# State-space mixer: front and output of a batch in pieces, one to a state; an own PSUM bank for rows of B; exponentials kept in du

## The chip, the cores and the metric

The kernel runs on one core of a Trainium2 chip. The metric is the device time of one execution in microseconds (us). The kernel is a chain of eight layers; the change lies in the seventh, a state-space mixer (`l3_attn`), and in the first step of the eighth.

## The reference

Input is x of shape 8 x 512 x 256 (batch, time, width), float32. Each layer computes `x = x + layernorm(f(layernorm(x)))`. For the seventh layer f is a selective state-space mixer with 512 channels and 16 states:

```
xr = x @ W_in.T                      # 256 -> 2 x 512
u, res = xr[..., :512], xr[..., 512:]
u = silu(causal_conv4(u) + b_conv)   # per channel
dt, B, C = split(u @ W_xproj.T, 16, 16, 16)
delta = softplus(dt @ W_dt.T + b_dt)
A = -exp(A_log)
for t:                               # per channel d and state n
    h = exp(delta*A) * h + delta*B*u
    y[d] = sum_n h[d, n] * C[n]
y = (y + u*D) * silu(res)
f = y @ W_out.T
```

The eighth layer is a mixture of experts whose routing starts with the layernorm of every batch of x.

## The kernel before

All activations lie with 128 partitions. In the mixer channels are on partitions in four chunks c, and the 512 times of a batch lie along the free axis. The loop runs over `order`, the pairs (batch b, state n), 8 x 16. For each pair:

- ACT writes `dA = exp(delta*A)` for each chunk into one of two PSUM banks (`pA`, L1727),
- DVE scans over time, `h = dA*h + dB` (L1730), into one of six buffers of two chunks,
- POOL multiplies h by the row of C, in place, two chunks at a time (L1733),
- PE adds h into the four banks `py` with an identity matrix (`summed`, L1701); this is issued one state late.

`dB = du*B`, where du = delta*u, is made two states ahead by `inputs`. For even states PE spreads the row of B over the partitions with a matmul into PSUM (`pb`, L1673) and DVE multiplies (L1676). For odd states a DMA on SP's queue brings the row from DRAM (L1680) and POOL multiplies (L1681). The row of C always comes by DMA (L1670).

`front(b)` makes what a batch needs. Its steps are the norm (`norm_act`, ACT writes xn, L160; PE transposes it, L146), four times a projection (`project_in`, `pi`, L1609), copy to `xc` (L1620), convolution by matmuls with diagonal matrices (`pc`, L1623) and bias (L1626), then Silu of u (L1628), the projection to dt, B and C (L1633), softplus in four chunks (ACT L1651 to L1655, DVE L1657 to L1659), and du on POOL (L1662). It is a generator: one step is issued behind each state of the batch before, and the rest ahead of state 14.

The boundary between batches is in state 0 of the next one. There stand the gate of the batch that has ended (`gate`, DVE, L1691), the first term of y (L1739), the output projection and the residual (`out`: `project_out`, L193, and `add_norm`), and the projections and Silu of the next `sr = silu(res)` (L1745, L1746). In `add_norm` DVE takes statistics (L105, L107, L113 to L115, L170), ACT normalizes (L177) and POOL adds to X (L182).

Two PSUM banks (`pmm`) serve the norm's transposes, projections, convolutions, softplus, rows of B and the output projection; two hold dA and four y. The instructions of an engine run in their order. That order is set by a scheduler, which takes the program's order as priority but moves work forward when by its own estimate it is ready. So work of the next layer can stand inside the mixer: the statistics of routing do (`norm` with L105, L118, L90 to L96).

Of the kernel before, what the change touches and what calls it, by code (L numbers as in the profile page):

```python
# [45 lines left out]
class Kern:  # L46


    def __init__(self, ctx, tc, i):
        self.ctx, self.tc, self.nc, self.i = ctx, tc, tc.nc, i  # L50
        nc = self.nc
        self.const = ctx.enter_context(tc.tile_pool(name="const", bufs=1))
        self.xpool = ctx.enter_context(tc.tile_pool(name="xres", bufs=1))
        self.wpool = ctx.enter_context(tc.tile_pool(name="wts", bufs=1))
        self.small = ctx.enter_context(tc.tile_pool(name="small", bufs=3))
        self.dram = ctx.enter_context(tc.tile_pool(name="dram", bufs=1, space=DRAM))
        self.C = self.const.tile([P, 384], F32, name="C")
        nc.sync.dma_start(out=self.C, in_=i["consts"][:, 0:384])
        self.ident = self.C[:, C_ID:C_ID + 128]
        self.caus = self.C[:, C_CAUS:C_CAUS + 128]  # L60
        self.up = self.C[:, C_UP:C_UP + 128]
        self.ones = self.const.tile([1, 128], F32, name="ones")
        nc.vector.memset(self.ones, 1.0)
        self.XA = self.xpool.tile([P, NB, NT, D], F32, name="X")
        self.X = [self.XA[:, b] for b in range(NB)]
        self.W = {}

        self.log_exp = False
        self.eps = self.const.tile([P, 1], F32, name="eps")
        nc.vector.memset(self.eps, LN_EPS)  # L70
# [55 lines left out]
    def norm(self, b, pool):  # L126

        nc = self.nc
        x = self.X[b]
        mv, r = self.stats([x[:, n, :] for n in range(NT)], "ln")  # L130
        xn = pool.tile([P, NT, D], F32, tag="xn", name=f"xn{b}")
        for n in range(NT):
            nc.vector.tensor_scalar(
                xn[:, n, :], x[:, n, :], mv[:, n, 0:1], r[:, n:n + 1], ALU.subtract, ALU.mult)
        return xn
# [15 lines left out]
    def norm_act(self, b, pool):  # L151

        nc = self.nc
        x = self.X[b]
        mv, r = self.stats([x[:, n, :] for n in range(NT)], "ln")
        nb = self.small.tile([P, NT], F32, tag="lnb", name="lnb")
        nc.vector.scalar_tensor_tensor(nb, mv[:, :, 0], -1.0, r, ALU.mult, ALU.mult)
        xn = pool.tile([P, NT, D], F32, tag="xn", name=f"xn{b}")
        for n in range(NT):
            nc.scalar.activation(  # L160
                xn[:, n, :], x[:, n, :], AF.Identity, bias=nb[:, n:n + 1], scale=r[:, n:n + 1])
        return xn

    def add_norm(self, b, ys, pool, tag="yn", halves=(), parts=1):
# [6 lines left out]
        t = pool.tile([P, NT, D], F32, tag=tag, name=f"yn{b}")  # L171
# [1397 lines left out]
def l3_attn(K):  # L1569

    nc, tc = K.nc, K.tc
# [5 lines left out]
    with ExitStack() as es:  # L1579
# [4 lines left out]
        pmm = pool("pm", 2, space=PSUM)  # L1584
# [21 lines left out]
        def project_in(b, c, xT):  # L1606
            ps = pmm.tile([P, L], F32, tag="mm", name=f"pi{b}_{c}")
# [6 lines left out]
        def front(b, res):  # L1614
            xT = K.norm_T(
                b, s1, pmm, "mm", xn=K.norm_act(b, s1), dst=s1.tile([P, 2, L], F32, tag="xT", name=f"xT{b}"))
            yield
            u = s1.tile([P, 4, L], F32, tag="u", name=f"u{b}")
            for c in range(4):
                nc.scalar.copy(xc[:, 3:], project_in(b, c, xT))  # L1620
# [5 lines left out]
                nc.scalar.activation(u[:, c, :], pc, AF.Identity, bias=W[:, c, M_BC:M_BC + 1])  # L1626
                yield
            nc.scalar.activation(flat(u), flat(u), AF.Silu)  # L1628
            K.log_exp_tables()
            yield  # L1630
# [12 lines left out]
            dl = s2.tile([P, 4, L], F32, tag="dl", name=f"dl{b}")  # L1643
            for c in range(4):
                ps = pmm.tile([P, L], F32, tag="mm", name=f"pd{b}_{c}")
# [3 lines left out]
                e = s2.tile([P, L], F32, tag="e", name=f"e{b}_{c}")  # L1649
                lg = s2.tile([P, L], F32, tag="lg", name=f"lg{b}_{c}")  # L1650
                nc.scalar.activation(e, ps, AF.Abs, bias=bd)  # L1651
                nc.scalar.activation(dl[:, c, :], ps, AF.Relu, bias=bd)
                nc.scalar.activation(e, e, AF.Exp, scale=-1.0)
                nc.scalar.activation(ps, e, AF.Identity, bias=1.0)
                nc.scalar.activation(lg, ps, AF.Ln)  # L1655

                nc.vector.scalar_tensor_tensor(ps, ps, -1.0, e, ALU.add, ALU.subtract)  # L1657
                nc.vector.tensor_tensor(ps, lg, ps, ALU.subtract)
                nc.vector.tensor_tensor(dl[:, c, :], ps, dl[:, c, :], ALU.add)  # L1659
                yield  # L1660
            du = s2.tile([P, 4, L], F32, tag="du", name=f"du{b}")
            nc.gpsimd.tensor_tensor(flat(du), flat(dl), flat(u), ALU.mult)  # L1662
            res.update(xT=xT, u=u, dl=dl, du=du, xd=xd,
                       rows=xd_d.rearrange("(j n) t -> n j t", j=2))

        def inputs(b, n):
            du, xd, rows = res[b]["du"], res[b]["xd"], res[b]["rows"]
            dB = s3.tile([P, 4, L], F32, tag="dB", name=f"dB{b}_{n}")
            C = s4.tile([P, L], F32, tag="C", name=f"C{b}_{n}")
            nc.sync.dma_start(out=C, in_=rows[n, 1].partition_broadcast(P))  # L1670
            if n % 2 == 0:
                pb = pmm.tile([P, L], F32, tag="mm", name=f"pb{b}_{n}")
                nc.tensor.matmul(  # L1673
                    pb, lhsT=K.ident[0:48, 16 + n:17 + n].to_broadcast([48, P]), rhs=xd,
                    start=True, stop=True)
                nc.vector.tensor_tensor(  # L1676
                    dB, du, pb[:, None, :].to_broadcast([P, 4, L]), ALU.mult)
            else:
                B = s2.tile([P, L], F32, tag="B", name=f"B{b}_{n}")
                nc.sync.dma_start(out=B, in_=rows[n, 0].partition_broadcast(P))  # L1680
                nc.gpsimd.tensor_tensor(  # L1681
                    dB, du, B[:, None, :].to_broadcast([P, 4, L]), ALU.mult)
            return dB, C

        def out(b, yT):
            K.project_out(
                b, [(yT[:, c, :], W[:, c, M_OUT:M_OUT + D]) for c in range(4)], pmm, "mm", s1, tag="xn")
# [16 lines left out]


# [5 lines left out]
        ready = {k: inputs(*k) for k in order[:2]}  # L1711
        py = sr = last = None
        nxt = iter(())
        for k, (b, n) in enumerate(order):
            if n == 0:
                nxt = front(b + 1, res[b + 1]) if b + 1 < NB else iter(())
                dl, u = res[b]["dl"], res[b]["u"]
            if n == NS - 2:
                for _ in nxt:
                    pass  # L1720
            dB, C = ready.pop((b, n))
            if k + 2 < len(order):
                ready[order[k + 2]] = inputs(*order[k + 2])
            hs = []
            for c in range(4):
                dA = pA.tile([P, L], F32, tag="dA", name=f"dA{b}_{n}_{c}")
                nc.scalar.activation(dA, dl[:, c, :], AF.Exp, scale=A[:, c, n:n + 1])  # L1727
                if c % 2 == 0:
                    hs.append(s6.tile([P, 2, L], F32, tag="h", name=f"h{b}_{n}_{c}"))
                nc.vector.tensor_tensor_scan(  # L1730
                    hs[-1][:, c % 2, :], dA, dB[:, c, :], 0.0, ALU.mult, ALU.add)
            for h in hs:
                nc.gpsimd.tensor_tensor(h, h, C[:, None, :].to_broadcast([P, 2, L]), ALU.mult)  # L1733
            summed(last)
            if n == 0:
                yT = gate(b - 1, py, sr) if b else None
# [4 lines left out]
                if b:  # L1741
                    out(b - 1, yT)
                sr = s1.tile([P, 4, L], F32, tag="sr", name=f"sr{b}")
                for c in range(4):
                    nc.scalar.copy(sr[:, c, :], project_in(b, 4 + c, res[b]["xT"]))  # L1745
                nc.scalar.activation(flat(sr), flat(sr), AF.Silu)  # L1746
                K.log_exp_tables()
            last = (py, hs, n)
            next(nxt, None)
        summed(last)  # L1750
        out(NB - 1, gate(NB - 1, py, sr))
# [4 lines left out]
def l3_ffn(K):  # L1756
# [18 lines left out]
    with ExitStack() as es:  # L1775
# [60 lines left out]
        def route(b, sb):  # L1836

            xn = K.norm(b, sb)
# [343 lines left out]
```

## Time and profile before

| what | value |
|---|---|
| median of 3 runs (lowest, highest) | 5109.19 us (5106.86, 5115.65) |
| profiled execution, its time | 5105.01 us |
| its span | 5103.3 us |
| granted TensorE clock, mean | 0.933 |
| mixer, from the first scan to the last matmul of y | 3346.9 to 4447.1 us |
| POOL, DVE, PE busy between 3343 and 4437 us | 918, 838, 932 us of 1094 |

A line of the groups has line, engine, operation, result and operands, count, then busy time and mean ns of one, and the idle time just ahead of it with what ended that. A line of a timeline has start, length, engine, line, operation, count, and in brackets the idle time ahead of it with its releaser. A line of waits has who waited for whom, the sum in us, how many times, and the longest.

### The profile page before, as it was taken

The numbers are of one execution on the slowest core, as the hardware profiler recorded it, in microseconds if no ns is written. First come the engines' busy times: TensorE is split into PE (matmuls) and PEld (weight loads), VectorE is DVE, ScalarE is ACT, GpSimd is POOL, SyncE is SP. The second block draws the span as 40 slices with busy tenths as digits, with TensorE's granted clock in tenths as the row PEclk, the third lists the DMA queues.
The fourth block names the chain that finished last, engine by engine and source line by source line (L and its number), as shares of the span: only waits on it lengthen the run. The fifth ranks groups of instructions, "written<-read, shape, count | busy, mean of one in ns | idle before, by whom it ended". The sixth has DMA issues, their size and how long they took to land.

```text
span 5103.3 us, 56570 instructions
## 1 busy us (share of the span) xinstructions
PE 4394.7 (86%) x18804; PEld 2694.8 (53%) x18804; DVE 3045.6 (60%) x8229; ACT 1958.5 (38%) x3835; POOL 1854.5 (36%) x1209
## 2 busy tenths in 40 slices
PE   8745788999895698899999999888888888799998
PEld 3334675555553697455555555433333333368884
DVE  6999746465778212666666543277777787751115
ACT  5411333434333233444444434365455555421112
POOL 0001212444433343211111110078778888803321
PEclk9877898999998899899999999999999999999999
DMA  4287421000001696000000000011111111126763
GB/s 114 79 198 177 130 64 56 5 5 9 5 14 40 171 249 173 5 5 5 5 5 5 1 21 1 1 54 45 42 44 44 50 46 42 56 71 226 235 206 103
DMA packets 401528, 357.89 MB, mean 70 GB/s; under 512 B 209394, under 2 KB 334020, under 8 KB 400676
## 3 DMA queue, kind: packets, MB, share of 16 engines
q1 hardware_dynamic: 373236, 305.83, 21.6%
q0 software_dynamic: 16320, 31.65, 2.2%
q10 hardware_dynamic: 11680, 16.80, 1.0%
q8 instruction: 149, 2.44, 0.2%
q14 instruction: 143, 1.17, 0.1%
HBM read 287.87 MB, written 66.09 MB: 69 GB/s over the span
## 4 chain that ended last, share of the span: by engine, by line
PE 37%; DVE 18%; issue 4%; POOL 4%; ACT 3%; DMA 1%; DVEq 0%; POOLq 0%; ACTq 0%; SPq 0%
DVE h L1730 7%; PE T L1432 5%; PE gb L1809 4%; DVE junk L1402 3%; PE h L1243 3%; PE g L1558 3%; PE y L1701 3%; PE yb L1823 2%; PE py L193 2%; DVE dB L1676 2%; PE pc L1623 2%; PE y L1254 2%; POOL h L1733 2%; PE o L1422 2%; PE pi L1609 1%
## 5 line engine op out<-in xcount | busy, mean ns | idle before, releaser
L1733 POOL TENSOR_TENSOR h<-h,C 128x1024 f32<-128x1024 f32 x256 | 595.8, 2354 | 175.6 <-DVE h L1730 141.9
L1701 PE MATMUL y<-h,C 128*128 128x512 f32 x1024 | 531.4, 660 | 107.1 <-POOL h L1733 107.1
L1730 DVE TENSOR_TENSOR_SCAN h<-dA,dB 128x512 f32<-128x512 f32 x512 | 589.0, 1203 | 29.4 <-ACT dA L1727 11.7
L1727 ACT ACTIVATE dA<-dl,A 128x512 f32<-128x512 f32 x512 | 352.5, 691 | 410.8 <-DVE h L1730 404.7
L1701 PEld LDWEIGHTS y<-h,C 128*128 128x128 f32 x1024 | 201.2, 208 | 414.5 <-issue 222.3
L938 POOL TENSOR_SCALAR p<-p,rs 128x128 f32<-128x128 f32 (+3 forms) x256 | 276.0, 1087 | 385.5 <-DVE rs L937 225.9
L1435 ACT ACTIVATE PT<-T 128x256 f32<-128x256 f32 (+3 forms) x512 | 212.1, 438 | 416.1 <-PE T L1432 396.0
L182 POOL TENSOR_TENSOR X<-X,yn 128x1024 f32<-128x1024 f32 (+1 forms) x80 | 154.1, 1932 | 590.3 <-ACT yn L177 529.3
L1397 PE MATMUL S<-KT,qz 128*128 128x512 f32 (+3 forms) x1024 | 326.0, 455 | 38.4 <-ACT qz L1385 16.9
L1432 PE MATMUL T<-qz,KT 128*128 128x512 f32 (+3 forms) x1024 | 318.1, 447 | 6.3 <-DVE mx L1402 4.2
L1437 POOL TENSOR_SCALAR_AFFINE_SELECT PT<-PT 128x512 f32<-128x512 f32 x128 | 81.8, 640 | 604.2 <-ACT PT L1435 599.8
L1681 POOL TENSOR_TENSOR dB<-du,B 128x2048 f32<-128x2048 f32 x64 | 289.6, 4525 | 0.1
L1402 DVE CUSTOM_DVE_ANT_0 junk<-S,mask 128x256 f32<-128x256 f32 (+3 forms) x512 | 249.8, 488 | 46.7 <-PE S L1397 2.6
L1397 PEld LDWEIGHTS S<-KT,qz 128*128 128x128 f32 x1024 | 178.5, 191 | 158.8 <-DVE mx L1402 36.7
L1809 PE MATMUL gb<-xbT,w_b 128*128 128x256 f32 (+1 forms) x1472 | 255.3, 332 | 1.0 <-ACT ts L2013 0.6
L1676 DVE TENSOR_TENSOR dB<-du,pb 128x2048 f32<-128x2048 f32 x64 | 145.4, 2273 | 167.2 <-PE pb L1673 117.5
L1815 DVE TENSOR_TENSOR hTb<-sb,gb 128x512 f32<-128x512 f32 x71 | 48.8, 687 | 325.4 <-PE gb L1809 325.4
L1809 PEld LDWEIGHTS gb<-xbT,w_b 128*128 128x128 f32 x1472 | 230.2, 191 | 23.1 <-ACT ts L2013 0.8
L1432 PEld LDWEIGHTS T<-qz,KT 128*128 128x128 f32 x1024 | 168.2, 191 | 121.5 <-issue 70.4
L936 ACT ACTIVATE p<-p,nm 128x128 f32<-128x128 f32 (+3 forms) x256 | 143.8, 563 | 198.5 <-DVE nm L932 193.3
L1248 ACT ACTIVATE hT<-h,w_l_ffn 128x128 f32<-128x128 f32 x384 | 109.8, 368 | 220.4 <-PE h L1243 220.4
L1243 PE MATMUL h<-xgT,w 128*128 128x128 f32 x1536 | 185.0, 279 | 0.0
(505 smaller groups left out, 9125.8 us busy)
## 6 DMA issues: line engine op xcount, KB each, us to landing
w_b<-l3f_w SPq DMA_DIRECT2D x138, 512.0 KB
w<-l1f_w SPq DMA_DIRECT2D x48, 1024.0 KB
C<-xdd SPq DMA_DIRECT2D x128, 256.0 KB
B<-xdd SPq DMA_DIRECT2D x64, 256.0 KB
w<-l1f_w SPq DMA_DIRECT2D x48, 256.0 KB
toep<-l0fd SPq DMA_DIRECT2D x32, 320.0 KB
X<-x SPq DMA_DIRECT2D x16, 512.0 KB
toep<-l0fd SPq DMA_DIRECT2D x32, 256.0 KB
```

The costliest lines, as they stand in the source:

```text
L938: nc.gpsimd.tensor_scalar(p[:, 0:n], p[:, 0:n], rs, None, ALU.mult)
L1243: nc.tensor.matmul(ph[:, j, :], lhsT=w1[:, s, c, m * P:(m + 1) * P], rhs=xgT[:, c, :], start=(c == 0), stop=(c == 1))
L1397: nc.tensor.matmul(ps[:, 0:n], lhsT=QZ[:, j, qt * P:n], rhs=KT[:, g, 0:n], start=True, stop=True)
L1402: nc.vector.tensor_tensor_reduce(out=junk[:, 0:n], in0=tiles[j][:, 0:n], in1=mask[:, L - n:L], scale=1.0, scalar=-3.0e38, op0=ALU.add, op1 ...
L1432: nc.tensor.matmul(ps[:, 0:n], lhsT=KT[:, g, kt * P:(kt + 1) * P], rhs=QZ[:, j, kt * P:L], start=True, stop=True)
L1676: nc.vector.tensor_tensor(dB, du, pb[:, None, :].to_broadcast([P, 4, L]), ALU.mult)
L1681: nc.gpsimd.tensor_tensor(dB, du, B[:, None, :].to_broadcast([P, 4, L]), ALU.mult)
L1701: nc.tensor.matmul(py[2 * j + c], lhsT=K.ident, rhs=h[:, c, :], start=False, stop=(n == NS - 1))
L1727: nc.scalar.activation(dA, dl[:, c, :], AF.Exp, scale=A[:, c, n:n + 1])
L1730: nc.vector.tensor_tensor_scan(hs[-1][:, c % 2, :], dA, dB[:, c, :], 0.0, ALU.mult, ALU.add)
L1733: nc.gpsimd.tensor_tensor(h, h, C[:, None, :].to_broadcast([P, 2, L]), ALU.mult)
L1809: nc.tensor.matmul(ps[:, q, :], lhsT=ww[:, k, (c + q) * P:(c + q + 1) * P], rhs=xT[:, k, :], start=(k == 0), stop=(k == 1))
```

## The change

Front and output of a batch are cut into 15 pieces, and one is issued in each of the states 1 to 15, between the second and the third scan (`among`). Pieces 1 to 5 are the norm, projections and convolutions; 6 is both Silu and the projection to dt, B and C; 7 to 12 softplus and du; 13 and 15 the projections for `sr`. The output of the batch before goes into pieces 7, 9 and 10. In state 0 only the gate and the first term of y are left.

`pmm` has one bank; the other becomes `pB`, for rows of B, half of the softplus projections, the `sr` projections and the halves of the output. Rows are asked for three states ahead (`rows_of`), and the products are made two ahead (`product`). The exponentials of softplus are kept in the place of du, so Abs and Exp of all chunks come ahead of the logarithms, and du is then written over them in four parts. xn lies in half of u. `sr` has two buffers, and its Silu is taken together with that of the next u. In the last batch the pieces take the statistics of routing for batches 0 to 6, each held on DVE behind a `fence`, and `norm` in the eighth layer uses them.

```diff
+    def fence(self):
+        t = self.small.tile([P, 1], F32, tag="fence", name="fence")
+        return self.tc.keep_in_program_order(self.nc.vector.memset(t, 0.0)).ins
-    def norm(self, b, pool):
+    def norm(self, b, pool, known=None):
-        mv, r = self.stats([x[:, n, :] for n in range(NT)], "ln")
+        mv, r = known or self.stats([x[:, n, :] for n in range(NT)], "ln")
...
-        pmm = pool("pm", 2, space=PSUM)
+        pmm = pool("pm", 1, space=PSUM)
+        pB = pool("pb", 1, space=PSUM)
...
-        def front(b, res):
+        def front(b, res, sr=None):
+            u = s1.tile([P, 4, L], F32, tag="u", name=f"u{b}")
+            xn = K.norm_act(b, s1, u[:, 2:4, :].rearrange("p c t -> p (c t)").rearrange(
+                "p (n d) -> p n d", n=NT))
             xT = K.norm_T(
+                b, s1, pmm, "mm", xn=xn, dst=s1.tile([P, 2, L], F32, tag="xT", name=f"xT{b}"))
+            nc.scalar.copy(xc[:, 3:], project_in(b, 0, xT))
             yield
             for c in range(4):
-                nc.scalar.copy(xc[:, 3:], project_in(b, c, xT))
                 pc = pmm.tile([P, L], F32, tag="mm", name=f"pc{b}_{c}")
...
+                if c < 3:
+                    nc.scalar.copy(xc[:, 3:], project_in(b, c + 1, xT))
                 yield
-            nc.scalar.activation(flat(u), flat(u), AF.Silu)
+            for t in (sr, u):
+                if t is not None:
+                    nc.scalar.activation(flat(t), flat(t), AF.Silu)
             K.log_exp_tables()
-            yield
...
             for c in range(4):
-                ps = pmm.tile([P, L], F32, tag="mm", name=f"pd{b}_{c}")
+                pl, tag = (pmm, "mm") if c < 2 else (pB, "pb")
+                ps = pl.tile([P, L], F32, tag=tag, name=f"pd{b}_{c}")
...
-                nc.scalar.activation(e, ps, AF.Abs, bias=bd)
+                nc.scalar.activation(du[:, c, :], ps, AF.Abs, bias=bd)
                 nc.scalar.activation(dl[:, c, :], ps, AF.Relu, bias=bd)
-                nc.scalar.activation(e, e, AF.Exp, scale=-1.0)
-                nc.scalar.activation(ps, e, AF.Identity, bias=1.0)
+                if c % 2:
+                    e = flat(du[:, c - 1:c + 1, :])
+                    nc.scalar.activation(e, e, AF.Exp, scale=-1.0)
+                if c == 1:
+                    yield
+            for c in range(4):
+                ps = pmm.tile([P, L], F32, tag="mm", name=f"pl{b}_{c}")
+                lg = s1.tile([P, L], F32, tag="e", name=f"lg{b}_{c}")
+                nc.scalar.activation(ps, du[:, c, :], AF.Identity, bias=1.0)
                 nc.scalar.activation(lg, ps, AF.Ln)
+                yield
-                nc.vector.scalar_tensor_tensor(ps, ps, -1.0, e, ALU.add, ALU.subtract)
+                nc.vector.scalar_tensor_tensor(ps, ps, -1.0, du[:, c, :], ALU.add, ALU.subtract)
                 nc.vector.tensor_tensor(ps, lg, ps, ALU.subtract)
                 nc.vector.tensor_tensor(dl[:, c, :], ps, dl[:, c, :], ALU.add)
-                yield
-            nc.gpsimd.tensor_tensor(flat(du), flat(dl), flat(u), ALU.mult)
+                nc.gpsimd.tensor_tensor(du[:, c, :], dl[:, c, :], u[:, c, :], ALU.mult)
+            for c in range(4):
+                if c % 2 == 0:
+                    yield
+                    if c:
+                        yield
+                nc.scalar.copy(res["sr"][:, c, :], project_in(b, 4 + c, xT, pB, "pb"))
...
+        def product(b, n, B):
+            dB = s3.tile([P, 4, L], F32, tag="dB", name=f"dB{b}_{n}")
+            m = 4 if n else 1
+            for c in range(0, 4, m):
+                (nc.gpsimd if n % 2 else nc.vector).tensor_tensor(
+                    dB[:, c:c + m, :], res[b]["du"][:, c:c + m, :],
+                    B[:, None, :].to_broadcast([P, m, L]), ALU.mult)
+            return dB
...
         def out(b, yT):
-            K.project_out(
-                b, [(yT[:, c, :], W[:, c, M_OUT:M_OUT + D]) for c in range(4)], pmm, "mm", s1, tag="xn")
+            t = s1.tile([P, NT, D], F32, tag="xn", name=f"yn{b}")
+            for half in range(2):
+                ps = pB.tile([P, 2, D], F32, tag="pb", name=f"po{b}_{half}")
...
+                nc.scalar.copy(t[:, 2 * half:2 * half + 2, :], ps)
+                yield
+            K.add_norm(b, [t[:, n, :] for n in range(NT)], s1, t=t)
...
+        def among(b, yT):
+            sr = res[b]["sr"]
+            behind = out(b - 1, yT) if b else iter(())
+            if b + 1 < NB:
+                for n, _ in enumerate(front(b + 1, res[b + 1], sr), 1):
+                    if n in (7, 9, 10):
+                        next(behind, None)
+                    yield
+            else:
+                for _ in behind:
+                    yield
+                nc.scalar.activation(flat(sr), flat(sr), AF.Silu)
+                K.log_exp_tables()
+                for d in range(NB - 1):
+                    yield
...
+                    with tc.issue_after(K.fence()):
+                        m, t = K.stats([K.X[d][:, n, :] for n in range(NT)], "ln")
+                        nc.vector.tensor_copy(mv, m)
+                        nc.vector.tensor_copy(r, t)
...
         for k, (b, n) in enumerate(order):
-            if n == NS - 2:
-                for _ in nxt:
-                    pass
-            if k + 2 < len(order):
-                ready[order[k + 2]] = inputs(*order[k + 2])
             for c in range(4):
...
+                if n and c == 1:
+                    next(nxt, None)
+                    if n == NS - 1:
+                        for _ in nxt:
+                            pass
+            if k + 2 < len(order):
+                ahead = order[k + 2]
+                dBs[ahead] = product(*ahead, rows[ahead][0])
+            if k + 3 < len(order):
+                rows[order[k + 3]] = rows_of(*order[k + 3])
...
             if n == 0:
...
-                if b:
-                    out(b - 1, yT)
-                sr = s1.tile([P, 4, L], F32, tag="sr", name=f"sr{b}")
-                for c in range(4):
-                    nc.scalar.copy(sr[:, c, :], project_in(b, 4 + c, res[b]["xT"]))
-                nc.scalar.activation(flat(sr), flat(sr), AF.Silu)
-                K.log_exp_tables()
+                nxt = among(b, yT)
```

## The prediction

> **What bounds the kernel now.** I read the page first (groups, idle times), then the waits inside the mixer (3343 to 4437 us), then the timelines of POOL and DVE over one boundary between two batches. Only the state-space mixer and the first microseconds after it are touched; the rest of the span is taken over unchanged.
>
> The groups (busy, mean ns | idle before, releaser):
>
> ```profile
> L1733 POOL TENSOR_TENSOR h<-h,C 128x1024 f32<-128x1024 f32 x256 | 595.8, 2354 | 175.6 <-DVE h L1730 141.9
> L1730 DVE TENSOR_TENSOR_SCAN h<-dA,dB 128x512 f32<-128x512 f32 x512 | 589.0, 1203 | 29.4 <-ACT dA L1727 11.7
> L1681 POOL TENSOR_TENSOR dB<-du,B 128x2048 f32<-128x2048 f32 x64 | 289.6, 4525 | 0.1
> ```
>
> POOL's work for one batch is 595.8/8 + 289.6/8 + 4.5 (du) + 2.35 (adding to X) = 117.5 us. DVE's: 64 scans at a pitch of 1.13 are 72, eight products at 2.2 are 18, softplus 8, gate 2.5, statistics with their waits about 5: 105. PE's, at full clock: 232 matmuls of 512 columns at 0.43, 32 of 256 at 0.215: 107. A batch takes, from one first gate to the next (DVE timeline):
>
> ```profile
> 3471.65 0.69 DVE L1691 TENSOR_TENSOR sr<-y,sr 128x512 f32<-128x512 f32 x1 [1.60 <-PE y L1701]
> ...
> 3615.53 0.69 DVE L1691 TENSOR_TENSOR sr<-y,sr 128x512 f32<-128x512 f32 x1 [1.59 <-PE y L1701]
> ```
>
> 143.9 us; over the six periods up to the gate at 4331.94 it is 143.4. So POOL is the nearest bound and idles 26 us a batch. Where, its timeline says:
>
> ```profile
> 3624.72 9.28 POOL L1733 TENSOR_TENSOR h<-h,C 128x1024 f32<-128x1024 f32 x4
> 3636.77 4.65 POOL L1733 TENSOR_TENSOR h<-h,C 128x1024 f32<-128x1024 f32 x2 [2.77 <-DVE onb L170]
> 3641.37 2.36 POOL L182 TENSOR_TENSOR X<-X,yn 128x1024 f32<-128x1024 f32 x1
> 3643.68 4.54 POOL L1681 TENSOR_TENSOR dB<-du,B 128x2048 f32<-128x2048 f32 x1
> 3666.36 9.28 POOL L1733 TENSOR_TENSOR h<-h,C 128x1024 f32<-128x1024 f32 x4 [18.14 <-DVE h L1730]
> ```
>
> 18.1 of the 26.4 us are one hole just behind the boundary, in which POOL waits for a scan. DVE over the same stretch:
>
> ```profile
> 3643.76 1.41 DVE L105 BATCH_NORM_STATS2 lnst<-X 128x6 f32<-128x256 f32 x4 [4.92 <-POOL X L182]
> 3646.84 1.39 DVE L115 SCALAR_TENSOR_TENSOR lnw<-lnh,lny 128x4 f32<-128x4 f32 x1 [1.66 <-ACT xn L160]
> ...
> 3661.46 2.29 DVE L1676 TENSOR_TENSOR dB<-du,pb 128x2048 f32<-128x2048 f32 x1 [12.01 <-PE pb L1673]
> 3663.79 9.02 DVE L1730 TENSOR_TENSOR_SCAN h<-dA,dB 128x512 f32<-128x512 f32 x8
> ```
>
> DVE waits 4.92 us for X (statistics that belong to the next layer's routing, pulled forward by the scheduler), 1.66 for xn, and 12.01 for the row of B, whose matmul stands on PE behind projections, transposes and the first convolution, all sharing two PSUM banks. The waits of the mixer in total:
>
> ```profile
> POOL h L1733 <- DVE h L1730: 141.9, 28, 18.2
> ...
> DVE dB L1676 <- PE pb L1673: 117.5, 17, 16.3
> ...
> DVE dB L1676 <- POOL du L1662: 49.7, 8, 6.4
> DVE lnst L105 <- POOL X L182: 29.5, 6, 4.9
> ```
>
> **The change, part by part.** (1) Rows of B get the bank pB and are asked for three states ahead, not two. This takes away most of the 12.0 us and the later waits for pb (3.9 us at 3676). A two-pass pb matmul costs 0.86 us as before. (2) Projections, convolutions, softplus and output projection become pieces 1 to 15, one behind the second scan of each state. Instruction counts on PE stay; ACT gains two copies of the output halves (2 x 0.58) and loses two table loads a batch (2 x 1.28). Its 72 us a batch stay beside the scans. (3) du becomes four products of 128x512 in pieces 9 to 12: POOL's 128x512 add to X costs 1.26 elsewhere, so 4 x 1.26 = 5.0 against 4.5: +0.5 on POOL. The 6.4 us that DVE waits for du go, since product (b+1, 0) is due only in state 14. (4) Both Silu in piece 6: 1.28 + 1.91 + 1.91 + 1.28 = 6.4 us in one block on ACT, against 4.5 now. DVE holds two dA ahead (2.3 us), so it stops up to 4 us; POOL behind it has a state of finished scans. (5) SP: the same number of row DMAs, C now needs a fourth buffer of four; a late C stops only transfers that are due three states later. On POOL's queue the du pieces stand between h products, 1.26 each.
>
> What is late next? Left at a boundary: the gate's wait for PE (3 us on DVE a boundary), 0.6 for ony, and POOL's 2.77 behind the output statistics. The stretch in which the front already runs one piece a state (3666 to 3737, about ten states) shows 4.1 us of POOL idle (1.51, 1.11, 1.47), 0.4 a state. So I take idle of 2.8 + 4.1 + 2.2 more for pieces and the Silu block: 117.5 + 0.5 + 9 = 127, and for the six periods 126.5. The first batch, which has the front's pieces and no boundary, supports it: 3346.9 to 3471.7, 124.8 us. **Six periods: 6 x 16.9 = -101.** Bounds: no idle but the gate (120: -140), and a boundary half kept (134: -56).
>
> (6) Last batch. Statistics of routing for batches 0 to 6 are now seven pieces in states 4 to 10, each behind a fence on DVE. The nearest row is the set behind the output projection: 3628.30 to 3636.59 is 8.3 us, less three scans of 1.13, is 4.9 us of DVE. Of it, 2.2 is one four-element operation:
>
> ```profile
> 3631.80 2.22 DVE L113 SCALAR_TENSOR_TENSOR onh<-onmv,ony 128x4 f32<-128x4 f32 x1 [0.60 <-ACT ony L112]
> ```
>
> It ends with POOL's block of four (3624.72 + 9.28 = 3634.0). Elsewhere, two POOL products stand back to back, and two such DVE operations end each with one of them:
>
> ```profile
> 3017.21 2.53 POOL L182 TENSOR_TENSOR X<-X,yn 128x512 f32<-128x512 f32 x2 [14.73 <-ACT yn L177]
> ```
> ```profile
> 3017.29 1.24 DVE L95 TENSOR_TENSOR lnw<-lnw,lny 128x4 f32<-128x4 f32 x1
> ...
> 3019.12 0.64 DVE L96 SCALAR_TENSOR_TENSOR lny<-lnw,lny 128x4 f32<-128x4 f32 x1
> ```
>
> The Trainium skill ("SBUF — State Buffer", section "SBUF: two separate sides") gives the rule: DVE and GpSimd share a port pair that is locked for a whole instruction; a DVE operation with two SBUF inputs, or in a two-port mode, takes it too. It speaks against the change, since it adds five such operations a set (three with two inputs, two copies). By the rule at its worst each waits out a POOL product: 2.6 + 5 x 2.35 = 14.4 us a set, 100 in all. By the row, one wait a set: 4.9 + 0.3 for copies and fence, 36 in all. I take the row: once DVE is late, POOL runs out of scans and leaves the lock, as the 2.77 shows. DVE then needs 72 + 15 + 2.5 + 4.9 + 36 = 131 in the last period, which takes 112.7 now and would be set by DVE: 133. **+20** (bounds 0, if ACT and POOL waits cover it, and +85, the rule's price).
>
> (7) Front of batch 0, covered by nothing: one bank makes each next projection wait for the evacuation, 3 x 1.0; softplus goes through one bank, 4 x 3.6 behind 8 us, against 17.5 now: +5; du and the first product in quarters let the first scan start before the last quarter, -6. **+2** (-6 to +10). (8) End: two copies before the output statistics +1; routing starts with its statistics known, but from 4464 on PE is busy 10 of 10 us there, so -2. **-1.**
>
> Sum: -101 + 20 + 2 - 1 = -80. The profiled execution took 5105.0 us (span 5103.3, 1.7 around it), which gives 5025. The median of the three runs is 4.2 above the profiled one: 5029.
>
> **Rivals.** *Slower: one bank stops PE.* PE works in order. With one bank for the front, in pieces 2 to 5 a projection waits until ACT has emptied the convolution, and that activation stands behind up to two dA, each tied to a scan at 1.13. The h matmuls behind it wait, h buffers (six, three states) stay full, scans stop, and POOL after them. PE has (126.5 - 107)/16 = 1.2 us spare a state, and less if its clock falls: in the holes the granted clock was 0.51 and 0.63 in 6-us windows. The 80 us gained are gone at 80/105 = 0.8 us lost in each of the 105 states that carry a piece; at 1.5 us it is +158, about 5187. For it: a piece of two hand-overs is new, and piece 8 asks for pB in an even state, where the row of B still holds it. Against: 0.4 a state in the stretch that has such pieces now.
>
> *Half the gain.* The lock costs its full price in the last batch and in each output norm, period 134 and last period +40: -56 + 40 + 1, about 5094. For it: the rule; against: the row.
>
> *More gain.* Idle nearly gone (period 120, -140) and statistics hidden but for +5: about 4975. For it: POOL runs 9.28 and 13.8 us blocks without a gap in mid-batch. Against: DVE and PE are close behind POOL.
>
> *It doesn't happen.* The scheduler orders by its own estimate, not as written (the statistics of routing inside the mixer show it), so the holes could stay where they are: about 5105.
>
> **How the numbers follow.** Likeliest 0.50 at 5029, its own range 4985 to 5080; more gain 0.15; half 0.13; slower 0.19; unchanged 0.03. About 10 us (0.2%) is what a measurement of this kernel can tell from no change. Faster 0.78, same 0.03, slower 0.19. The range goes down to 4970, which leaves out half of the larger gain, and up to 5125, which leaves out most of the slower case.
>
> **What would show it.** Right: POOL's longest wait for a scan under 6 us; dB's wait for pb under 30 in total, for du near 0; first gates 122 to 131 us apart; the last period longer than 120 with four-element DVE operations of 2 us in it. Wrong: matmuls of h waiting for ACT through the projections; scans waiting for dA or for h buffers by tens of microseconds; periods over 140.

## The result and the profile after

The changed kernel is slower by 0.3%: 5124.19 us (median of 9 runs, 5120.81 to 5129.41) against 5106.86 for the kernel before (9 runs). The ratio on record is 1.0029, with an interval of 1.0021 to 1.0037; the two medians alone give 1.0034. The prediction of 5029 was wrong, though its range ended only just above the result. The profiled execution took 5125.25 us, its span 5123.5.

The stages of the mixer, from the DVE and POOL timelines of both kernels. The head runs from the last addition to X of the sixth layer to the first scan; a period runs from one first gate to the next.

| stage, us | before | after | predicted change | measured change |
|---|---|---|---|---|
| head | 68.9 | 74.9 | +2 | +6.0 |
| first batch | 124.8 | 144.4 | 0 | +19.6 |
| six periods | 860.3 | 822.8 | -101 | -37.5 |
| last period | 112.7 | 136.9 | +20 | +24.2 |
| sum | 1166.7 | 1179.0 | -79 | +12.3 |

Behind the last gate 2.1 us more are spent (-1 predicted). The remaining 5.8 us of the 20.2 between the two spans lie ahead of the mixer, where the order of instructions on every engine is the same in both kernels. In the profiles of this study the mixer's head begins anywhere from 3274.8 to 3289.0 us, so this part is taken as variation from run to run.

First the groups of the page after (busy, mean ns | idle before, releaser):

```profile
L1797 DVE TENSOR_TENSOR_SCAN h<-dA,dB 128x512 f32<-128x512 f32 x512 | 594.1, 1204 | 140.5 <-PE y L1748 99.9
L1810 POOL TENSOR_TENSOR h<-h,C 128x1024 f32<-128x1024 f32 x256 | 597.2, 2353 | 168.7 <-DVE h L1797 114.3
L1716 POOL TENSOR_TENSOR dB<-du,B 128x2048 f32<-128x2048 f32 x64 | 289.2, 4518 | 0.1
```

Busy times and means are those of before, and POOL's idle time nearly so, 168.7 against 175.6. What is new is on the scan's line: DVE idles 140.5 us there instead of 29.4, mostly for PE's `y` (99.9, where it was 2.9). A scan that waits for `y` waits for an h buffer that PE has not yet summed. The waits of the mixer after (3343 to 4460 us) say the same, and show what the change did remove:

```profile
POOL h L1810 <- DVE h L1797: 114.3, 52, 9.4
...
DVE h L1797 <- PE y L1748: 99.9, 31, 9.6
...
DVE dB L1716 <- PE pb L1704: 23.4, 16, 2.2
```

The wait for rows of B fell from 117.5 us to 23.4. The 18-us hole is gone, but POOL now waits 52 times instead of 28. The gates, from the DVE timeline:

```profile
3639.53 2.48 DVE L1738 TENSOR_TENSOR sr<-y,sr 128x512 f32<-128x512 f32 x4
```
```profile
3783.16 2.48 DVE L1738 TENSOR_TENSOR sr<-y,sr 128x512 f32<-128x512 f32 x4
```

In both gates all four parts run without a wait. Before, the seven gates ahead of the last waited for PE 21 times, 21.1 us in all; after, they do not wait. Yet the period between the two takes 143.6 us, as before. The six are 136.5, 143.6, 144.4, 132.2, 133.1 and 133.0. The second and third are long and the last three short, with different causes; the first lies between and is not taken apart here.

**A long period.** Timelines of POOL, DVE, ACT and PE after, behind the gate at 3639.5, in order of start:

```profile
3647.21 9.28 POOL L1810 TENSOR_TENSOR h<-h,C 128x1024 f32<-128x1024 f32 x4
3651.94 9.03 DVE L116 SCALAR_TENSOR_TENSOR lnw<-lnh,lny 128x4 f32<-128x4 f32 x1
3656.45 4.49 POOL L1716 TENSOR_TENSOR dB<-du,B 128x2048 f32<-128x2048 f32 x1
3660.89 1.21 DVE L1797 TENSOR_TENSOR_SCAN h<-dA,dB 128x512 f32<-128x512 f32 x1
3665.70 5.33 PE L1638 MATMUL pc<-xc,dg 128*128 128x512 f32 x8 [9.54 <-ACT xc L1633]
3674.78 2.34 DVE L1797 TENSOR_TENSOR_SCAN h<-dA,dB 128x512 f32<-128x512 f32 x2 [8.15 <-PE y L1748]
3677.29 2.35 POOL L1810 TENSOR_TENSOR h<-h,C 128x1024 f32<-128x1024 f32 x1 [8.00 <-DVE h L1797]
```

A DVE operation on four elements in each partition, the last of the norm's statistics, takes 9.03 us. It starts inside POOL's block of four products and ends with the dB behind the block, at 3660.9. Elsewhere it takes 0.13; here it waits for the port pair that DVE shares with POOL (the lock of the prediction). From there one can follow the delay. The scans stop, so ACT stops at its next dA, and the copy of the projection to `xc` stands behind that dA. PE waits 9.54 us for `xc` with the sums of h queued behind the convolution; the h buffers stay full, scans wait 8.15, and POOL 8.00.

**A short period.** Here the longest such operation takes 3.05 us. PE after, from 4084 to 4111 us:

```profile
4084.18 3.70 PE L1638 MATMUL pc<-xc,dg 128*128 128x512 f32 x8
4087.82 1.12 PE L1704 MATMUL pb<-xd,C 48*128 48x512 f32 x2
4088.87 1.98 PE L1619 MATMUL pi<-xT,w_l_attn 128*128 128x512 f32 x4
4090.69 3.60 PE L1748 MATMUL y<-h,C 128*128 128x512 f32 x8
4094.12 3.60 PE L1638 MATMUL pc<-xc,dg 128*128 128x512 f32 x8
...
4107.62 3.70 PE L1748 MATMUL y<-h,C 128*128 128x512 f32 x8
```

PE is never idle here. A row of the windows view of the same kernel (PE, PEld, DVE, ACT, POOL busy, then the granted clock):

```profile
4074.00:4112.00 38.00, 37.42 (x84) 14.78 (x83) 22.06 (x18) 19.16 (x26) 34.52 (x13) 1.00 0.19 56
```

PE is busy 37.42 of 38.00 us at full clock, while POOL loses 3.48 us of it in one hole. A state with a convolution gives PE 8 passes for the sums of h, 8 for the taps, 4 for the projection and on average 1 for a row of B: 21 at a pitch of 0.43 make 9.0 us. POOL's two products (4.65) and half a dB (2.25) make 6.9. Four such states follow one another, and six h buffers hold three states.

**The last batch.** DVE and POOL timelines after, inside one of the seven sets of statistics:

```profile
4385.90 1.43 DVE L116 SCALAR_TENSOR_TENSOR lnw<-lnh,lny 128x4 f32<-128x4 f32 x1
4388.39 3.41 DVE L1775 COPY fr<-lnw 128x4 f32<-128x4 f32 x1
```
```profile
4384.96 2.35 POOL L1810 TENSOR_TENSOR h<-h,C 128x1024 f32<-128x1024 f32 x1 [1.57 <-DVE lnh L115]
4387.26 4.51 POOL L1716 TENSOR_TENSOR dB<-du,B 128x2048 f32<-128x2048 f32 x1
```

The two DVE operations end with POOL's product (4387.31) and with its dB (4391.77). In the whole mixer, 33 DVE operations on four or eight elements took more than 0.5 us each after, 87.8 us in all; before, it was 11, with 20.3 us. Every one of these 44 ends within 0.03 us behind the end of a POOL instruction. That is the evidence that it is POOL they wait for.

### The profile page after: what moved, and what is told of

Its sections match the earlier page's. It is cut to its first block, busy times and chain, and to the rows that moved or that the text cites. A ratio compares the mean times of both kernels' runs of the same rounds, so it can differ in the third digit from the quotient of the medians.

```text
span 5123.5 us, 56747 instructions
## 1 busy us (share of the span) xinstructions
PE 4411.6 (86%) x18804; PEld 2700.7 (53%) x18804; DVE 3101.1 (61%) x8204; ACT 1974.8 (39%) x3853; POOL 1857.7 (36%) x1233
## 5 line engine op out<-in xcount | busy, mean ns | idle before, releaser
L1797 DVE TENSOR_TENSOR_SCAN h<-dA,dB 128x512 f32<-128x512 f32 x512 | 594.1, 1204 | 140.5 <-PE y L1748 99.9
L1810 POOL TENSOR_TENSOR h<-h,C 128x1024 f32<-128x1024 f32 x256 | 597.2, 2353 | 168.7 <-DVE h L1797 114.3
L1405 PE MATMUL S<-KT,qz 128*128 128x512 f32 (+3 forms) x1024 | 326.5, 456 | 36.9 <-ACT qz L1393 16.9
L1440 PEld LDWEIGHTS T<-qz,KT 128*128 128x128 f32 x1024 | 168.7, 192 | 122.5 <-issue 71.0
L1256 ACT ACTIVATE hT<-h,w_l_ffn 128x128 f32<-128x128 f32 x384 | 109.5, 368 | 220.8 <-PE h L1251 220.8
L1251 PEld LDWEIGHTS h<-xgT,w 128*128 128x128 f32 x1536 | 178.3, 194 | 0.0
```

What stands on the lines that cost most here:

```text
L1251: nc.tensor.matmul(ph[:, j, :], lhsT=w1[:, s, c, m * P:(m + 1) * P], rhs=xgT[:, c, :], start=(c == 0), stop=(c == 1))
L1405: nc.tensor.matmul(ps[:, 0:n], lhsT=QZ[:, j, qt * P:n], rhs=KT[:, g, 0:n], start=True, stop=True)
L1440: nc.tensor.matmul(ps[:, 0:n], lhsT=KT[:, g, kt * P:(kt + 1) * P], rhs=QZ[:, j, kt * P:L], start=True, stop=True)
L1797: nc.vector.tensor_tensor_scan(hs[-1][:, c % 2, :], dA, dB[:, c, :], 0.0, ALU.mult, ALU.add)
```

## The experiments

Each kernel changes the one named in its paragraph. Kernels e1 to e4 ran beside the kernel before at 5110.02 us, e5 to e8 at 5109.47, e9 to e12 at 5108.75; all ratios are against that.

**e1: the small DVE operations taken away.** In `stats` the Newton step goes, and the negated mean and the copies that are kept go to ACT:

```diff
-            nc.scalar.activation(y, y, AF.Exp, scale=-0.5)
-            nc.vector.scalar_tensor_tensor(t, var, LN_EPS, y, ALU.add, ALU.mult)
-            nc.vector.scalar_tensor_tensor(t, t, -0.5, y, ALU.mult, ALU.mult)
-            nc.vector.scalar_tensor_tensor(r, t, 1.5, y, ALU.add, ALU.mult)
+            nc.scalar.activation(r, y, AF.Exp, scale=-0.5)
...
-        nc.vector.scalar_tensor_tensor(nb, mv[:, :, 0], -1.0, r, ALU.mult, ALU.mult)
+        if self.log_exp:
...
+            nc.scalar.activation(m, mv[:, :, 0], AF.Identity, scale=-1.0)
+            for n in range(NT):
+                nc.scalar.activation(
+                    nb[:, n:n + 1], m[:, n:n + 1], AF.Identity, scale=r[:, n:n + 1])
...
-                        nc.vector.tensor_copy(mv, m)
-                        nc.vector.tensor_copy(r, t)
+                        nc.scalar.copy(mv, m)
+                        nc.scalar.copy(r, t)
```

> The changed kernel with no DVE operation of two SBUF inputs left in the mixer: the inverse root is taken from ACT alone (its Newton step on DVE is left out), the bias of the norm and the copies of the kept statistics are made on ACT. Theory (DVE is held by POOL's lock): the two waits of 9.0 and 9.3 us go, periods of 143.6 and 144.3 us fall to 133, the last period from 137 to about 117, output norms give back 3 us a batch: 20 + 21 + 18, about -59, 5065 us. Rival (PE's order alone sets the periods): the last period falls, the six periods stay within 3 us: about -25, 5099 us.

5050.54 us, ratio 0.9881 (0.9865 to 0.9898): 74 us below the changed kernel, and below the kernel before. The six periods fall to 783.8, all of them between 127.8 and 132.4, and the last from 136.9 to 108.0. The theory held and was a little small. The waits of e1 (3280 to 4470 us) also show what stays:

```profile
DVE h L1808 <- PE y L1759: 78.7, 21, 5.2
POOL h L1821 <- DVE h L1808: 72.8, 43, 5.2
```

The longest waits are down from 9.6 and 9.4 to 5.2, but scans still wait 78.7 us for PE.

**e2: no statistics of routing in the last batch.** The loop over `d` in `among` is left out, so that `norm` takes all its own statistics.

```diff
-                for d in range(NB - 1):
...
-                    with tc.issue_after(K.fence()):
-                        m, t = K.stats([K.X[d][:, n, :] for n in range(NT)], "ln")
...
```

> The changed kernel without the seven pieces of routing statistics in the last batch; the eighth layer takes its own, as before the change. Theory: the last period falls from 137 to about 117 us, the start of the eighth layer loses 2 to 4, so about -17, 5107 us. Rival: the scheduler pulls the statistics back into the mixer, where they wait for X on DVE as before the change (4.9 us in six periods): +10 us or more, 5134 us.

5118.7 us, ratio 1.0017 (1.0008 to 1.0026). The last period falls by 27.4 us, to 109.5, but the six periods rise by 20.4, to 843.2. The DVE timeline of e2, ahead of a gate, says why:

```profile
3634.62 3.98 DVE L119 TENSOR_SCALAR lnv<-lnmv 128x4 f32<-128x4 f32 x1
3638.64 2.27 DVE L91 TENSOR_SCALAR lny<-lnv 128x4 int32<-128x4 int32 x1
3640.82 2.38 DVE L93 TENSOR_SCALAR lnh<-lnv 128x4 f32<-128x4 f32 x1
```

The scheduler pulls the statistics of the eighth layer back among the scans, and three of its small operations alone take 8.6 us there. The last batch's cost is these operations, as the prediction had it, but leaving out their place only moves them.

**e3: PE's work cut.** From batch 1 on the convolution has one tap of its four; the other three are left out.

```diff
+                T = 1 if b else 4
...
-                for s in range(4):
+                for s in range(T):
```

> The changed kernel with one convolution tap instead of four from batch 1 on (three of four taps are left out): 24 matmuls of 0.43 us less a batch in pieces 2 to 5, 10.3 us of PE. Theory (h matmuls stand behind the pieces' matmuls on PE, scans wait for h buffers): scans' waits for y fall from 100 us to under 50, each of seven periods loses about 8 us: -55, 5069 us. Rival (the lock on DVE sets them): the waits of 9 us stay and the time falls by less than 15.

5053.91 us, ratio 0.9883 (0.9867 to 0.99). The scans' wait for PE, in the same view as above:

```profile
DVE h L1798 <- PE y L1749: 35.2, 33, 4.7
```

It falls from 99.9 to 35.2 us, the six periods by 57.8 us, the first batch by 10.1. The last period, which carries no convolution, stays at 136.9. The theory held, and the gain of 70 us was larger than the 55 expected. The matmuls that were left out cost time nearly one for one: 24 passes a batch at 0.43 us are 10.3, and a period fell by 9.6.

**e4: sums ahead of the piece.** `summed(last)` is issued behind the second scan, ahead of the piece, so that PE frees h buffers first.

```diff
+                if c == 1:
+                    summed(last)
                 if n and c == 1:
                     next(nxt, None)
...
-            summed(last)
```

> The changed kernel with the matmuls that sum h issued ahead of the state's piece instead of behind it. Theory (PE's order): scans' waits for y fall by half, about -40, 5084 us. Rival: PE now waits for POOL's product ahead of the piece, and the piece is late: 0 to +40 us.

5095.89 us, ratio 0.9966 (0.9955 to 0.9977), 28 us below the changed kernel, where 40 were expected. The first batch falls by 13.4, and the long periods of 143.6 and 144.4 become 136.8 and 136.6; the short ones stay at 133. The DVE timeline of e4 shows why the long periods are shorter:

```profile
3639.25 3.38 DVE L116 SCALAR_TENSOR_TENSOR lnw<-lnh,lny 128x4 f32<-128x4 f32 x1 [0.77 <-ACT u L167]
```

The operation that took 9.03 us now takes 3.38, and no small operation of the mixer takes more than 3.92 (60.0 us in 23, instead of 87.8 in 33). So the order on PE changed the wait for the lock itself. Whether it also shortens what follows such a wait, e4 does not tell apart.

**e5: the edit of e1 on the kernel before.** The control: is e1's gain simply that of leaving work out?

> The kernel before with the same edit as the first experiment: no DVE operation of two SBUF inputs in the mixer's norms (Newton step of the inverse root left out, bias on ACT). A control. Theory: the lock matters when POOL has a backlog, which it hardly has at the old boundary, where each batch shows one wait of 2.1 us and at most one of 1.4: about 2 us in each of seven periods, -15, 5095 us. Rival: leaving out the Newton step and its round trip is worth what the first experiment won by itself: -50 or more, 5060 us.

5104.35 us, ratio 0.9993 (0.9985 to 1.0002): no difference. The six periods measure 856.4 instead of 860.3. There was also less to take away: small operations over 0.5 us fall from 11 (20.3 us) to 6 (13.7 us, those of the eighth layer's routing, which the edit leaves). In the old order DVE had to wait for the row of B in any case, and POOL, empty during that wait, held no lock. The edit gains 74 us only where the change has filled POOL's queue. A kernel that keeps the operations but frees them of the lock was not run; that the 74 us are the lock's rests on their lengths and on where they end.

**e6: the bank for rows of B on the kernel before.** Only this part of the change: one bank left for the front, the other for rows of B and the second half of the output.

```diff
-        pmm = pool("pm", 2, space=PSUM)
+        pmm = pool("pm", 1, space=PSUM)
+        pB = pool("pb", 1, space=PSUM)
...
-                pb = pmm.tile([P, L], F32, tag="mm", name=f"pb{b}_{n}")
+                pb = pB.tile([P, L], F32, tag="pb", name=f"pb{b}_{n}")
...
```

> The kernel before with one part of the change alone: rows of B in a bank of their own, one bank left for the front; the second half of the output projection goes through the bank of the rows. No pieces, rows still two states ahead. Theory: the wait of dB for its row falls from 117 us to under 50, periods from 143 to about 136, the first front 5 us later: -40, 5070 us. Rival: with one bank the front's steps hold PE and the rows wait behind them as before, now with h matmuls too: -5 to +40, 5125 us.

5136.51 us, ratio 1.0058 (1.0042 to 1.0075): slower by 27 to 30 us. Its waits (3280 to 4470 us):

```profile
POOL du L1663 <- DVE dl L1660: 117.9, 7, 75.4
POOL h L1744 <- DVE h L1741: 82.7, 43, 6.6
DVE h L1741 <- PE y L1712: 71.6, 23, 5.1
```

POOL's longest wait for a scan falls from 18.2 to 6.6 us and the sum from 141.9 to 82.7, which is what the prediction wanted. Even so the six periods are 869.9, not less than 860.3. Scans wait 71.6 us for PE instead of 2.9, and POOL has a new hole of up to 8.6 us a batch: it waits for the softplus of the next batch before it makes du (six times, 42.5 us; the 75.4 are the head's). The head grows by 15.6 us and the last period by 14.2, while the first batch falls by 10.1. So the row bank trades waits with no pieces and no new statistics, but only in part the same ones as the change: that one gives softplus a second bank, and there POOL waits for softplus only in batch 0.

**e7 and e8: the sums first, and the output's statistics late, on e1.** e7 is e1 with the edit of e4; e8 also puts a fence on DVE ahead of the statistics of the output.

```diff
-            K.add_norm(b, [t[:, n, :] for n in range(NT)], s1, t=t)
+            with tc.issue_after(K.fence()):
+                K.add_norm(b, [t[:, n, :] for n in range(NT)], s1, t=t)
```

> The first and the fourth experiment together: no DVE operation of two SBUF inputs in the mixer (Newton step left out), and the sums of h ahead of the piece. If the gains are of two kinds, the first batch falls from 137 to about 128 us and the periods of 131 by 1 to 2: about -18 against the first experiment, 5033 us. If the fourth only shortened the waits for the lock, no change: 5050 us.

> As the seventh, and the statistics of the output norm held on DVE behind a fence at piece 10, so that DVE does not wait for the copy of an output half in the middle of its scans (4.7 us in each of six periods). Theory (that wait stops POOL by 3 us a period): -15 to -20 against the seventh. Rival: POOL has the slack, no change within 5 us.

5052.0 (0.9887, 0.987 to 0.9903) and 5051.48 (0.9889, 0.9872 to 0.9905): both as e1 in total. The stages differ, though. In e7 the first batch falls by 10.1 us, as the theory said, and the six periods rise by 15.3, to 799.1: five of them are 133.0 or 133.1 us. So the order on PE moves time between stages even without the small operations. Of this, 5 us are work of POOL that passes with the gate from the first batch to the periods (busy 119.6 us in the first batch instead of 124.8); the rest is not explained. e8's periods are those of e7 (799.6), so the wait behind the output's statistics is slack there.

**e9: both causes taken away.** e1 with the one tap of e3.

> The version without the statistics' small DVE operations on SBUF (5050.5), and the convolution of batches 1 to 7 with one tap of its four; work left out: three taps, and the Newton step. Theory: two separate costs add: DVE waiting for the lock in the statistics, and PE's own work in the states that carry a convolution (8 sums of h, 8 passes of the taps, 4 of the projection, 0.45 us each). So the six periods go from 131 to about 122.5 and the first batch from 137 to 127: 5050 - 51 - 10 = 4990. Rival: PE was only late because the evacuation of the projection stood behind DVE's lock waits; then, without those, the taps cost nothing, and it stays within 10 us of 5050.

4981.06 us, ratio 0.9754 (0.9737 to 0.977). The theory held and was again small. The four kernels make a square:

| us | four taps | one tap |
|---|---|---|
| small DVE operations there | 5124.2 | 5053.9 |
| taken away | 5050.5 | 4981.1 |

The operations are worth 73.7 and 72.8 us, the taps 70.3 and 69.4. Worked out from the ratios to the kernel before instead, whose intervals are 4 to 8 us either way, they are 76 and 66, 75 and 65. So they add to within some 10 us: these are two causes and not one seen twice. From e1 to e9 the six periods fall from 783.8 to 719.3, 10.75 us a period, for 10.3 us of matmuls left out. POOL's timeline in e9, in the first of the states with a convolution:

```profile
3869.86 9.28 POOL L1822 TENSOR_TENSOR h<-h,C 128x1024 f32<-128x1024 f32 x4
3879.11 4.50 POOL L1728 TENSOR_TENSOR dB<-du,B 128x2048 f32<-128x2048 f32 x1
3883.57 9.29 POOL L1822 TENSOR_TENSOR h<-h,C 128x1024 f32<-128x1024 f32 x4
3892.82 4.53 POOL L1728 TENSOR_TENSOR dB<-du,B 128x2048 f32<-128x2048 f32 x1
```

POOL has no hole there, and this period takes 119.6 us with POOL busy for 117.2. That is the bound the prediction had aimed at, and it is reached only with both causes gone.

**e10: two banks for the front of batch 0.** e1, with convolution, step sizes and softplus of batch 0 alone spread over both banks.

```diff
...
-                ps = pmm.tile([P, L], F32, tag="mm", name=f"pl{b}_{c}")
+                pl, tag = (pmm, "mm") if b or c % 2 else (pB, "pb")
+                ps = pl.tile([P, L], F32, tag=tag, name=f"pl{b}_{c}")
```

> The version without the statistics' small DVE operations on SBUF (Newton step left out), and in the front of batch 0 alone the convolution goes to the second bank, and the step sizes and their softplus to both banks in turn. Theory: the front of batch 0 is longer than before by 6 us because its hand-overs go through one bank: last add to X to first scan goes from 72 to 66, nothing else changes, 5044. Rival: the bank isn't what it waits for (ACT and DVE run the same chain), 5050.

5041.37 us, ratio 0.9871 (0.9855 to 0.9888). This is the lowest time of a kernel with all the convolution, but its interval overlaps that of e1. The head did not fall to 66 but rose from 72.2 to 81.7, and the first batch fell from 137.1 to 125.3: together 2.3 us. The theory of the head failed, and whether e10 beats e1 stays undecided.

**e11 and e12: PE's work spread.** In e11 each convolution of e1 is cut into two pieces of two taps, and states 11 to 14 carry two pieces each; e12 adds the edit of e10.

```diff
                 for s in range(4):
+                    if s == 2:
+                        yield
...
-                if n and c == 1:
+                if n and (c == 1 or c == 3 and n in (11, 12, 13, 14)):
```

> The version without the statistics' small DVE operations on SBUF (Newton step left out), with each convolution cut into two pieces of two taps, so that it covers states 2 to 9; to make room, states 11 to 14 carry two pieces each, behind the second and behind the fourth scan. All matmuls are there. Theory: PE's work is uneven over the states: about 9.7 us in each of four states in a row with a convolution, where POOL needs 7.3, while PE idles in states 12 to 15; spread out, it is 7 to 8 us. The six periods go from 131 to about 124 and the first batch from 137 to 127: 5050 - 42 - 10 = about 5000. Rival: the four states with two pieces make ACT late (12.5 us of evacuations and softplus besides 11 of dA), scans wait there instead, and it is 5050 or above.

> The two before together: spread convolution, and two banks for the front of batch 0 (Newton step left out). Theory: both gains add, 4994. Rival: as in each alone.

5065.16 (0.9911, 0.9895 to 0.9928) and 5069.42 (0.9923, 0.9907 to 0.994): no gain on e1. e12 is slower; e11 is by its median, but its interval just touches e1's. In e11 the first batch falls by 9.1 us, the six periods rise by 16.9 and the last, which has no convolution, by 9.6 (not explained). POOL in e11, in the states with convolutions and then around the gate at 3756.8:

```profile
3785.74 4.51 POOL L1729 TENSOR_TENSOR dB<-du,B 128x2048 f32<-128x2048 f32 x1
3790.22 9.28 POOL L1823 TENSOR_TENSOR h<-h,C 128x1024 f32<-128x1024 f32 x4
...
3840.60 4.52 POOL L1729 TENSOR_TENSOR dB<-du,B 128x2048 f32<-128x2048 f32 x1
```
```profile
3755.39 2.35 POOL L1823 TENSOR_TENSOR h<-h,C 128x1024 f32<-128x1024 f32 x1 [2.08 <-PE y L1761]
...
3779.00 2.37 POOL L1823 TENSOR_TENSOR h<-h,C 128x1024 f32<-128x1024 f32 x1 [3.80 <-PE pb L1717]
3783.44 2.35 POOL L1823 TENSOR_TENSOR h<-h,C 128x1024 f32<-128x1024 f32 x1 [2.07 <-DVE h L1810]
```

Through the convolutions POOL has no hole for 59 us, so spreading PE's work did there what the theory said. But the projections of `sr`, which a short period of the changed kernel has on PE ahead of the gate, now come behind it (four groups from 3759.83 to 3771.86), and POOL loses 8 us there. There are more holes, 2.1 to 2.8 us long, in the states with two pieces. The periods are 132.3 to 135.6. Moving PE's work about is not enough as long as some states have too much of it.

## Why the prediction was wrong

**The first step that failed is PE's spare time:** "PE has (126.5 - 107)/16 = 1.2 us spare a state". It is an average over states with different work. In the four states with a convolution PE needs 9.0 us where POOL needs 6.9, so it is short by 2.1 a state while 12 others have time to spare. e3 and e9 show it by the price of the taps, 70 us in each. The forecast saw the same rival, with a mechanism that fits only in part: it had PE waiting for the evacuations of one bank. In the long period shown PE does wait for one, 9.54 us, but because the lock holds up the scans; in the convolution states of the short period it hardly waits, it works.

**The support for it was misread.** "0.4 a state in the stretch that has such pieces" came from 3666 to 3737 us of the kernel before. There PE had begun the first two of the four convolutions at 3656.69 and 3664.07, inside POOL's hole, which ended at 3666.36. A row of the windows view of the kernel before, over the hole (columns as above):

```profile
3648.22:3666.36 18.14, 17.88 (x47) 7.46 (x46) 5.96 (x14) 8.89 (x11) 0.01 (x1) 1.00 0.04 15
```

PE was busy 17.88 of the 18.14 us: the hole was PE's time to catch up. Taking away the wait that opened it did not take away the work that ran in it.

**The second step, and in the six periods the larger, is the price of the lock in mid-batch.** The Trainium skill's page "SBUF — State Buffer", section "SBUF: two separate sides", lets whichever of the two engines starts first hold the port pair for its whole instruction. The forecast priced this only for the last batch and there took the row; for the fronts and outputs it put "2.8 + 4.1 + 2.2" of idle. Its rival of half the gain charged the lock to each output norm, but no case charged it to the norm of the front, where the waits of 9 us are. Taking the small operations away gives back 39.0 us in the six periods, 28.9 in the last and 7.3 in the first (e1 against after). The six periods lie 63.5 us above the forecast, so 24.5 are left, which the taps more than cover (e1 to e9: 64.5). The rule's worst, one product a wait, was too small at 3651.94: that wait ran through parts of three POOL instructions. "POOL runs out of scans and leaves the lock" is true only once DVE is late enough; in front of a backlog of finished scans DVE waited 9 us for it.

**The first batch**, taken as 0, cost 19.6 us: 7.3 by the small operations, 7 to 10 by the taps (e9 against e1, e3 against after). The rest fits POOL's own work, which the prediction did not move. Between the first scan and the first gate POOL is busy 124.8 us after and 114.7 before: it makes nine products dB there instead of eight, 34 products of h instead of 32, and du in five quarters instead of one piece. With both causes gone (e9) this stage still takes 130.3 us, with POOL busy for 124.6 of them. The head's 6 us are not settled; in e10, with a second bank, head and first batch together won only 2.3.

**What was right.** The wait for pb fell to 23.4 ("under 30 in total"), the seven gates ahead of the last lost their waits, dB's wait for du fell from 49.7 to 2.3 (scans wait 6.4 more for it). The last period rose by 24.2, for the stated reason, where 20 was said (e1 and e2). The sign named for the slower rival, scans waiting for h buffers by tens of microseconds, came true, and so did "periods over 140", in two of six. Of the four rivals on the table, two happened at once: the lock at its price, and PE in front of the h buffers. With either one gone the changed kernel lies below the kernel before (5050.5 and 5053.9). For the small operations a control was run (e5). The one tap was not tried on the kernel before, so how much of the taps' 70 us is new with the change is not shown; PE was busy all through the hole there too.

What would beat both kernels follows from it. e1 does, by 1.2%, at the price of the Newton step; the same edit on the kernel before is worth nothing (e5). More h buffers, which might carry PE over four long states, were not tried.

## What to carry to other kernels

A hole on the bounding engine can be the time in which another engine catches up: before you close it, list what the others do inside it, and compare their work state by state with what the buffers between them hold, not as an average over the batch. When a change fills the queue of POOL, price again every small DVE operation that needs the shared port: what was free in the hole costs microseconds in front of a backlog. And when two causes are suspected, remove each alone and both together; here the four times showed that they add to within some 10 us.

## What was not expected of the hardware

A DVE operation that waits for the port pair is not always let in between two POOL instructions. With POOL's next work ready, one took 9.03 us, past two ends of POOL instructions, and was done only with the third; another, at 3795.58, took 9.31, past three. Nearly all others after the change ended with the POOL instruction under way, after 1.0 to 3.4 us. It was not only operations with two inputs that took long (the page quoted above also names two-port modes): copies of 128x4 took up to 3.41 us, and TENSOR_SCALAR operations on four elements, with one input, 2.27 to 4.00 in e2. What decides between a short and a long wait, these runs do not show.
